# Layer 3 of a graph stack: another order for sums, W_h and W_out products, values and reciprocals within a period

## The chip, the cores and the metric

One core of a Trainium2 chip runs the whole program. The metric is the device time of one execution in microseconds, the median of several runs. Names in the profile: PE is the matmul engine, PEld its weight loader, DVE the vector engine, ACT the scalar engine, POOL the general one, SP the engine that here only issues DMAs. A "q" behind a name (SPq, ACTq) is the engine's instruction sequencer.

## The reference

Four graph layers follow each other on x (32 batches, 512 nodes, 64 features). Each takes h = relu(layernorm(x)) and adds its result to x. Only layer 3 is touched:

```python
def gat_layer(x, graph, W, b):
    h = x @ W
    s = jnp.einsum('bnd,bmd->bnm', h, h) * graph
    s = jnp.where(s == 0.0, NEG_INF, s)
    a = jax.nn.softmax(s, axis=2)
    return jnp.einsum('bnm,bmd->bnd', a, h) + b

heads = jax.vmap(lambda W, b: gat_layer(flow_x, graph, W, b))(Wh, bh)   # 8 heads, 64 -> 128
cat = jnp.moveaxis(heads, 0, 2).reshape(B, N, H * D)
x = jax.nn.leaky_relu(cat, negative_slope=0.01)
out = gat_layer(x, graph, W_out, b_out)                                 # 1024 -> 64
return jax.nn.leaky_relu(out, negative_slope=0.01)
```

## The kernel before

Layer 3 runs as a chain of 144 units. A `Heads` unit is two heads of one batch (32 batches x 4 = 128 units); an `Out` unit is the second attention of two batches (16 units). A unit handles k = 0, 1 (its two heads, or its two batches) side by side, in the two halves of the 128 rows or columns of PE. The 512 nodes are cut into C = 4 blocks of 128, so a unit has four score blocks, r = 0 to 3.

The steps of a unit, each a method of `Pair`, `Heads` or `Out`, on the engine named:

- `scores(r)` (PE): the 128 x 512 scores of block r, for both k. They go to a PSUM tile of the pool `ps_s`, which has two buffers (tag "s").
- `maxima(r)` (DVE, two instructions): adds the mask, takes the minimum of the negative along the row, writes the negated scores to `p_att`. After r = 3 the four blocks' maxima of both k stand in `top`.
- `spread_out` (DVE transpose, four SP DMAs to DRAM) and `spread_in` (one SP DMA of 512 KB): the maxima come back as a row on all partitions, `topb`.
- `shift(r)` (POOL): subtracts `topb`. The scores are symmetric, so a shift by the column's maximum serves.
- `exps(r)` (ACT): the exponential. For odd r it goes to PSUM, into one of the two buffers of `ps_s` (`e_ps`).
- `join(r)` for r = 1, 3 (DVE): p[r] = e_ps + p[r-1]. It frees the buffer in `ps_s`.
- `totals` (PE, then ACT): products with ones give the sums of each column, in a tile of the pool `ps_m` (two buffers, tag "m"); ACT copies them to `tot`. `totals_out`: two DMAs, one on SP and one on ACT, bring the two parts into `parts`, 128 partitions x 16.
- `values(j)` (PE): products of p[j] with the features, accumulated over j in `av`, the one buffer of `ps_v`. Since p[1] and p[3] are joined, even blocks use differences of features (`less_next`).
- `recips` (DVE): adds the two parts and takes the reciprocal; `recips_out` and `recips_in` (SP) send it through DRAM to all partitions, `recb`.
- `normalize` (DVE): o = av * recb. It frees `av`.
- A `Heads` unit goes on with `y_pe` (the two products with W_h, two tiles of `ps_m`), `y_act` (ACT: 0.01 y + 0.01 b_h) and `y_dve` (DVE: the maximum of that and y + b_h), which is `cat`. Two `Heads` units' `cat` feed `Out.product(h)` (PE): one head's share of the product with W_out, accumulated in `gT_ps` over the eight heads; `keep_product` (ACT) copies it out.
- An `Out` unit goes on with `y_act` (bias), `back` (PE: four transposes into a tile of `ps_m`; ACT: 0.01 y - 1), `back_dve` (DVE: the maximum), `back_pool` (POOL adds x) and `store` (SP).
- Preparations for later units: `features` (ACT, with one DVE reduction), `make_hx` (PE transposes in `ps_m`, ACT copy), `make_g` (PE: two products in `ps_m`, ACT copies), `make_v`, `make_gs`, `judge_product`.

The order is written by hand. The method `period(t)` (lines 711 to 769) lists what period t does for several units: `unit(k)` is the unit k places behind the one that now makes its scores. Under `manual_schedule` (line 1266) every engine, SP included, runs its instructions in the order in which this list issues them; the framework adds the waits and chooses which buffer of a pool a tile gets. An engine whose next instruction waits runs nothing behind it.

So in one period unit 0 makes score blocks 2 and 3 and their maxima, unit -1 its blocks 0 and 1, unit 1 its shifts, exponentials and joins, unit 2 its sums, values and reciprocals, unit 3 its normalisation, unit 4 the W_h product or the output. A product with W_out at period t takes the `cat` that unit 4 makes in the same period (first head of two), or the period before.

Of the kernel before, what the change touches and what calls it, by code (L numbers as in the profile page):

```python
# [8 lines left out]
F32 = mybir.dt.float32  # L9
# [5 lines left out]
P = 128  # L15
# [7 lines left out]
def fast_form(  # L23
# [25 lines left out]
    nc = tc.nc  # L49
    B, N, F = x.shape  # L50
    C = N // P
# [8 lines left out]
    tiny = ctx.enter_context(tc.tile_pool(name="tiny", bufs=4))  # L60
# [54 lines left out]
    for k in range(2):  # L115
        rows = slice(k * F, (k + 1) * F)
# [199 lines left out]
    class Pair:  # L316
# [112 lines left out]
        def totals(self):  # L429
            ps = ps_m.tile([P, N], F32, name="tot_ps", tag="m")  # L430
            for e in range(2):
                for k in range(2):
                    q = (2 * k + e) * 32
                    nc.tensor.matmul(  # L434
                        ps[q : q + 32, :], lhsT=ones, rhs=self.p[2 * e + 1][:, k],
                        start=True, stop=True,
                    )
            self.tot = wk.tile([P, N], F32, name="tot", bufs=1)
            nc.scalar.copy(self.tot, ps)  # L439

        def totals_out(self):

            self.parts = tiny.tile([P, 2, 8], F32, name="parts")
            rows = self.tot.rearrange("(k e r) n -> k e r n", k=2, e=2)
            for e, queue in enumerate((nc.sync, nc.scalar)):
                queue.dma_start(
                    self.parts[:, e], rows[:, e, 0].rearrange("k (g i) -> k g i", i=8)
                )

        def recips(self):  # L450
            self.rec = tiny.tile([P, 8], F32, name="rec_flow")
# [217 lines left out]
    def any_zero():  # L669

        def across(src, rows, name):
            ps = ps_m.tile([P, P], F32, name=name, tag="m")
            n = src.shape[0]
            nc.tensor.transpose(ps[:rows, :n], src, ident[:n, :n])
            return ps[:rows, :n]

        own = tiny.tile([P, 1], F32, name="own")
        nc.vector.tensor_reduce(own, least, AX.X, OP.min)
        two = tiny.tile([1, 2], F32, name="two")
        nc.vector.tensor_reduce(two[:, 0:1], across(own, 1, "own_ps"), AX.X, OP.min)  # L680
        best = tiny.tile([B // 2, 2], F32, name="best")
        nc.vector.tensor_reduce(
            best,
            across(least_out, B // 2, "out_ps").rearrange("b (k f) -> b k f", k=2),
            AX.X, OP.max,
        )
        worst = tiny.tile([B // 2, 1], F32, name="worst")
        nc.vector.tensor_reduce(worst, best, AX.X, OP.min)
        nc.vector.tensor_reduce(
            two[:, 1:2], across(worst, 1, "worst_ps"), AX.X, OP.min  # L690
        )
        flag = tiny.tile([1, 1], F32, name="flag")
        nc.vector.tensor_reduce(flag, two, AX.X, OP.min)
        nc.vector.scalar_tensor_tensor(
            again, flag, 0.0, unsound, op0=OP.is_equal, op1=OP.max
        )
# [6 lines left out]
    def planned(units, products):  # L703

        class Nothing:
            def __getattr__(self, name):
                return lambda *args: None

        nothing = Nothing()

        def period(t):
            def unit(lag):
                return units[t - lag] if 0 <= t - lag < len(units) else nothing

            now, ahead = unit(0), unit(-1)
            for r in range(2, C):
                now.scores(r)
            unit(3).recips_in()
            unit(4).y_pe()
            unit(1).shift(0)  # L720
            unit(1).exps(0)
            unit(4).y_act()
            u, h = products.get(t - 1, (None, 0))
            if u and h == H - 1:
                u.keep_product()
            unit(1).shift(2)
            unit(1).exps(2)
            for r in range(2, C):
                now.maxima(r)
            now.spread_out()  # L730
            now.spread_in()
            for r in range(2):
                ahead.scores(r)
            unit(4).y_dve()
            unit(3).normalize()
            for r in range(2):
                ahead.maxima(r)
            unit(4).back()
            unit(2).totals()
            unit(2).totals_out()  # L740
            unit(1).shift(1)
            unit(1).exps(1)
            u, h = products.get(t, (None, 0))
            if u:
                u.product(h)
            for j in range(C):
                unit(2).values(j)
            unit(1).join(1)
            unit(1).shift(3)
            unit(1).exps(3)  # L750
            unit(5).back_pool()
            unit(-2).make_gs()
            unit(2).recips()
            unit(2).recips_out()
            unit(5).store()
            unit(4).back_dve()
            unit(1).join(3)
            unit(-3).features(3)
            unit(-2).judge_product()
            unit(1).make_v()  # L760
            unit(-4).make_hx()
            unit(-2).make_g()
            for step in range(3):
                for lag, odd in ((step - 7, 0), (step - 11, 1)):
                    u = unit(lag)
                    if getattr(u, "i", None) == 0 and u.b % 2 == odd:
                        u.features(step)
            if t == len(units):
                any_zero()

        return period
# [1067 lines left out]
```

## Time and profile before

| what | us |
|---|---|
| median of 3 runs | 2101.37 |
| range of the 3 runs | 2099.18 to 2102.93 |
| profiled execution | 2099.58 |
| its span, first to last instruction | 2097.8 |
| first and last of the 144 transposes `top_t` | 460.7 and 2053.4 |

The clock granted to PE is 0.985 over the span. The durations of the steps, from the groups of the page and of the list by shape:

| line | step | engine | count | mean ns of one |
|---|---|---|---|---|
| L382 | maxima, one k | DVE | 1152 | 685 |
| L404 | shift | POOL | 576 | 2374 |
| L413 | exps to SBUF, to PSUM | ACT | 288, 288 | 1056, 1028 |
| L416 | join | DVE | 288 | 1203 |
| L439 | copy of the sums | ACT | 144 | 586 |
| L452, L455 | reciprocals | DVE | 144, 144 | 170, 203 |
| L472 | normalize | DVE | 144 | 683 |
| L563 | y_act of a `Heads` unit, one k | ACT | 256 | 680 |
| L571 | y_dve, one k | DVE | 256 | 737 |
| L652 | back_dve | DVE | 16 | 644 |

How to read it: a row of the timeline has the start, the time until the end of the last of the merged instructions, engine, line, operation, what it writes and reads, the count, and in brackets the idle time before with what ended it. Matmuls overlap, so their rate is read from distances of starts, not from their durations. An fp32 product shows as two matmul instructions, so the two products of a step (k = 0, 1) are "x4". DVE's instructions overlap a little too: I use the distances of starts in sums. A row of the windows has the stretch, its length, the busy time of PE, PEld, DVE, ACT and POOL with the instruction counts, PE's clock, the DMA share and GB/s. Bytes a packet and times of packets are from the trace's DMA records.

### The profile page before, as it was taken

The numbers are of one execution on the slowest core, as the hardware profiler recorded it, in microseconds if no ns is written. First come the engines' busy times: TensorE is split into PE (matmuls) and PEld (weight loads), VectorE is DVE, ScalarE is ACT, GpSimd is POOL, SyncE is SP. The second block draws the span as 40 slices with busy tenths as digits, with TensorE's granted clock in tenths as the row PEclk, the third lists the DMA queues.
The fourth block names the chain that finished last, engine by engine and source line by source line (L and its number), as shares of the span: only waits on it lengthen the run. The fifth ranks groups of instructions, "written<-read, shape, count | busy, mean of one in ns | idle before, by whom it ended". The sixth has DMA issues, their size and how long they took to land. (4 is left out here: it accounts for less than half of the span.)

```text
span 2097.8 us, 33009 instructions
## 1 busy us (share of the span) xinstructions
PE 2002.6 (95%) x11038; PEld 813.8 (39%) x11038; DVE 1786.2 (85%) x4257; ACT 1227.9 (59%) x1944; POOL 1432.7 (68%) x697
## 2 busy tenths in 40 slices
PE   7999999988999999999999999999999999999995
PEld 4667676652333333333333333333333333333321
DVE  6699997667998989898989898989888888988983
ACT  3444443335666666666666666666666666766553
POOL 3000000018898889888888988888888888888995
PEclk9999999989999999999999999999999999999998
DMA  5000000001222222222222222222222222222222
GB/s 139 1 1 2 1 2 1 1 22 57 77 75 69 78 77 73 78 76 82 68 78 77 72 77 77 77 71 74 68 77 73 77 67 73 77 71 74 77 68 78
DMA packets 135780, 129.35 MB, mean 62 GB/s; under 512 B 92792, under 2 KB 98080, under 8 KB 135472
## 3 DMA queue, kind: packets, MB, share of 16 engines
q1 hardware_dynamic: 116368, 126.35, 19.8%
q10 hardware_dynamic: 18720, 0.59, 0.5%
q8 instruction: 89, 1.46, 0.3%
q0 software_dynamic: 512, 0.20, 0.1%
q14 instruction: 91, 0.75, 0.1%
HBM read 119.48 MB, written 5.37 MB: 60 GB/s over the span
## 5 line engine op out<-in xcount | busy, mean ns | idle before, releaser
L404 POOL TENSOR_TENSOR p_att<-p_att,topb 128x1024 f32<-128x1024 f32 x576 | 1347.4, 2374 | 232.7 <-DMA topb<-top_row 130.6
L382 DVE CUSTOM_DVE_ANT_0 p_att<-s_ps,flow_neg 128x512 f32<-128x512 f32 x1152 | 727.8, 685 | 53.6 <-PE s_ps L370 51.9
L370 PE MATMUL s_ps<-hx,g 64*128 64x512 f32 x2048 | 545.3, 615 | 34.3 <-DVE p_att L416 24.6
L413 ACT ACTIVATE e_ps<-p_att 128x1024 f32<-128x1024 f32 x288 | 295.8, 1028 | 174.2 <-DVE top L382 107.8
L413 ACT ACTIVATE p_att<-p_att 128x1024 f32<-128x1024 f32 x288 | 304.2, 1056 | 149.6 <-POOL p_att L404 146.6
L416 DVE TENSOR_TENSOR p_att<-e_ps,p_att 128x1024 f32<-128x1024 f32 x288 | 346.5, 1203 | 24.7 <-ACT e_ps L413 24.4
L370 PEld LDWEIGHTS s_ps<-hx,g 64*128 64x128 f32 x2048 | 179.4, 186 | 343.1 <-DVE top L382 163.2
L422 PE MATMUL av<-p_att,hd 128*64 128x512 f32 x1024 | 264.3, 593 | 2.2 <-DVE o_att L472 2.0
L422 PE MATMUL av<-p_att,hn 128*64 128x512 f32 x1024 | 263.7, 592 | 0.0
L1053 POOL TENSOR_TENSOR x<-x,bias_b 128x512 f32<-128x512 f32 x16 | 20.3, 1271 | 280.0 <-DVE hn L826 280.0
L571 DVE SCALAR_TENSOR_TENSOR cat<-y_ps,bh,cat 128x512 f32<-128x512 f32 x256 | 178.1, 737 | 6.2 <-ACT cat L563 3.4
L563 ACT ACTIVATE cat<-y_ps,bh 128x512 f32<-128x512 f32 x256 | 161.7, 680 | 11.8 <-PE y_ps L553 8.7
L434 PE MATMUL tot_ps<-p_att,ones 128*32 128x512 f32 x1152 | 154.8, 610 | 1.6 <-DVE cat L571 0.5
L553 PE MATMUL y_ps<-o_att,wh_sb 64*128 64x512 f32 x512 | 143.2, 589 | 0.0
L598 PE MATMUL gT_ps<-cat,wo_sb 128*64 128x512 f32 x512 | 138.1, 618 | 0.0
L439 ACT COPY tot<-tot_ps 128x512 f32<-128x512 f32 x144 | 84.4, 586 | 85.0 <-PE tot_ps L434 83.6
L422 PEld LDWEIGHTS av<-p_att,hd 128*64 128x64 f32 x1024 | 73.2, 137 | 152.2 <-issue 141.2
L422 PEld LDWEIGHTS av<-p_att,hn 128*64 128x64 f32 x1024 | 74.8, 137 | 144.9 <-issue 144.9
L472 DVE TENSOR_TENSOR o_att<-av,recb 128x512 f32<-128x512 f32 x144 | 98.3, 683 | 34.9 <-DMA recb<-rec_row 34.6
L547 ACT COPY g<-g_ps 128x512 f32<-128x512 f32 x128 | 70.3, 588 | 95.3 <-PE g_ps L535 95.3
L977 PE MATMUL acc<-v,s 64*128 64x65 f32 x2048 | 124.1, 280 | 0.7 <-DVE s L963 0.4
L977 PEld LDWEIGHTS acc<-v,s 64*128 64x128 f32 x2048 | 121.2, 195 | 5.9 <-DVE o L993 1.2
(181 smaller groups left out, 2028.2 us busy)
## 6 DMA issues: line engine op xcount, KB each, us to landing
topb<-top_row SPq DMA_DIRECT2D x144, 512.0 KB
recb<-rec_row SPq DMA_DIRECT2D x288, 128.0 KB
top_row<-top_t SPq DMA_DIRECT2D x576, 1.0 KB
out_dram<-y SPq DMA_DIRECT2D x32, 128.0 KB
x<-in_x_dram SPq DMA_DIRECT2D x3, 1024.0 KB
parts<-tot ACTq DMA_DIRECT2D x144, 4.0 KB
parts<-tot SPq DMA_DIRECT2D x144, 4.0 KB
rec_row<-rec_flow SPq DMA_DIRECT2D x144, 4.0 KB
```

Of the source, the lines that this page charges most:

```text
L370: nc.tensor.matmul(ps[:, k], lhsT=g[halves(k), r * P : (r + 1) * P], rhs=x[halves(k), :], start=True, stop=True,)
L382: nc.vector.tensor_tensor_reduce(out=self.p[r][:, k], in0=ps[:, k], in1=flow_neg[:, r], scale=-1.0, scalar=BIG, op0=OP.add, op1=OP.min, ac ...
L404: nc.gpsimd.tensor_tensor(self.p[r], self.p[r], self.topb, OP.subtract)
L413: nc.scalar.activation(to, self.p[r], AF.Exp, scale=-1.0)
L416: nc.vector.tensor_tensor(self.p[r], self.joined, self.p[r - 1], OP.add)
L422: nc.tensor.matmul(self.av[halves(k), :], lhsT=self.v(k, j) if j % 2 else self.less_next(k, j), rhs=self.p[j][:, k], start=(j == 0), stop= ...
L434: nc.tensor.matmul(ps[q : q + 32, :], lhsT=ones, rhs=self.p[2 * e + 1][:, k], start=True, stop=True,)
L553: nc.tensor.matmul(ps, lhsT=wh_sb[halves(k), 2 * self.i + k, :], rhs=self.o[halves(k), :], start=True, stop=True,)
L563: nc.scalar.activation(self.cat[:, k], self.y[k], AF.Identity, bias=bh01[:, h : h + 1], scale=0.01)
L571: nc.vector.scalar_tensor_tensor(self.cat[:, k], self.y[k], bh[:, h : h + 1], self.cat[:, k], op0=OP.add, op1=OP.max,)
L598: nc.tensor.matmul(self.gps[halves(k), :], lhsT=wo_sb[:, h, :], rhs=Heads.cat.pop((self.b + k, h)), start=(h == 0), stop=(h == H - 1),)
L977: nc.tensor.matmul(self.acc[k][:, r], lhsT=self.s[b // 2][halves(k), b % 2, r * P : (r + 1) * P], rhs=self.v[halves(k), b], start=(b == 0) ...
```

## The change

Only order changes, and `totals_out` is cut in two: it issues one of its two DMAs, on the queue that it is given; `parts` is allocated in `totals`.

- `totals` of unit 2 goes from behind unit 4's `back` to a place behind exps(0): on PE between the unit's own score blocks and the blocks ahead, on ACT between exps(0) and exps(2). Its ACT DMA follows directly; its SP DMA goes between `spread_out` and `spread_in`.
- `y_pe` of unit 4 goes behind the blocks ahead; `y_act` behind exps(2).
- `y_dve` goes behind the maxima ahead, so normalize and these maxima come before it; `back_dve` directly follows.
- `values` goes in front of the product with W_out.
- `recips` and `recips_out` go in front of join(1).

```diff
             self.tot = wk.tile([P, N], F32, name="tot", bufs=1)
+            self.parts = tiny.tile([P, 2, 8], F32, name="parts")
             nc.scalar.copy(self.tot, ps)
 
-        def totals_out(self):
-
-            self.parts = tiny.tile([P, 2, 8], F32, name="parts")
+        def totals_out(self, e, queue):
+
             rows = self.tot.rearrange("(k e r) n -> k e r n", k=2, e=2)
-            for e, queue in enumerate((nc.sync, nc.scalar)):
-                queue.dma_start(
-                    self.parts[:, e], rows[:, e, 0].rearrange("k (g i) -> k g i", i=8)
-                )
+            queue.dma_start(
+                self.parts[:, e], rows[:, e, 0].rearrange("k (g i) -> k g i", i=8)
+            )
...
             unit(3).recips_in()
-            unit(4).y_pe()
             unit(1).shift(0)
             unit(1).exps(0)
-            unit(4).y_act()
+            unit(2).totals()
+            unit(2).totals_out(1, nc.scalar)
             u, h = products.get(t - 1, (None, 0))
...
             now.spread_out()
+            unit(2).totals_out(0, nc.sync)
             now.spread_in()
             for r in range(2):
                 ahead.scores(r)
-            unit(4).y_dve()
+            unit(4).y_pe()
+            unit(4).y_act()
             unit(3).normalize()
             for r in range(2):
                 ahead.maxima(r)
             unit(4).back()
-            unit(2).totals()
-            unit(2).totals_out()
+            unit(4).y_dve()
+            unit(4).back_dve()
             unit(1).shift(1)
             unit(1).exps(1)
+            for j in range(C):
+                unit(2).values(j)
             u, h = products.get(t, (None, 0))
             if u:
                 u.product(h)
-            for j in range(C):
-                unit(2).values(j)
+            unit(2).recips()
+            unit(2).recips_out()
             unit(1).join(1)
...
             unit(-2).make_gs()
-            unit(2).recips()
-            unit(2).recips_out()
             unit(5).store()
-            unit(4).back_dve()
             unit(1).join(3)
```

## The prediction

> **What bounds the kernel now.** The page's first table comes first, then the waits, then the period on each engine (timeline and windows).
>
> ```profile
> PE 2002.6 (95%) x11038; PEld 813.8 (39%) x11038; DVE 1786.2 (85%) x4257; ACT 1227.9 (59%) x1944; POOL 1432.7 (68%) x697
> ```
>
> The layer runs from about 460 us to the end in 144 periods, one a DVE transpose `top_t`; the mean distance of two is 11.14 us. A period is a unit's four score blocks, so I work per period. The list of waits (total us, times, longest):
>
> ```profile
> POOL p_att L404 <- DMA topb<-top_row: 130.6, 88, 3.4
> PEld tot_ps L434 <- DVE cat L571: 100.7, 128, 1.1
> DVE rec_flow L452 <- DMA parts<-tot: 77.1, 118, 2.4
> DVE o_att L472 <- DMA recb<-rec_row: 34.6, 34, 4.9
> PEld s_ps L370 <- DVE p_att L416: 126.3, 156, 10.2
> ```
>
> The change aims at lines 2 to 4. The busy time by window, for four whole periods (columns: length, then PE, PEld, DVE, ACT, POOL):
>
> ```profile
> 1213.85:1224.70 10.85, 10.81 (x53) 3.57 (x52) 10.04 (x25) 6.39 (x9) 9.15 (x5) 1.00 0.23 75
> 1258.03:1268.51 10.48, 9.88 (x44) 2.71 (x44) 9.73 (x25) 7.13 (x12) 9.30 (x6) 1.00 0.23 79
> 1268.51:1281.14 12.63, 11.90 (x52) 4.03 (x52) 9.12 (x24) 8.30 (x16) 11.49 (x6) 1.00 0.23 72
> ```
>
> PE and DVE are both nearly full, POOL not far behind. So the large wait of 100.7 us needs a look at what PE did meanwhile. The timeline of PE:
>
> ```profile
> 1211.82 1.02 PE L553 MATMUL y_ps<-o_att,wh_sb 64*128 64x512 f32 x4
> 1212.74 2.26 PE L370 MATMUL s_ps<-gs 64*128 64x512 f32 x8
> 1214.93 1.07 PE L434 MATMUL tot_ps<-p_att,ones 128*32 128x512 f32 x8
> 1215.93 1.08 PE L598 MATMUL gT_ps<-cat,wo_sb 128*64 128x512 f32 x4
> 1216.84 1.03 PE L422 MATMUL av<-p_att,hd 128*64 128x512 f32 x4
> 1219.41 1.03 PE L422 MATMUL av<-p_att,hn 128*64 128x512 f32 x4
> 1220.37 0.66 PE L298 MATMUL hx_ps<-ident,hs 128*128 128x128 f32 x4
> 1220.95 1.99 PE L370 MATMUL s_ps<-gs 64*128 64x512 f32 x8
> ```
>
> Products of one shape follow at 0.86 us a pair (1216.84 to 1219.41 is three). Around `tot_ps` PE loses only 0.1 us a period: the 100.7 us are the weight loader's, hidden by the matmul before. What is open on PE are the steps between shapes and the score blocks' waits. The page's worst place is the period with `back` (an output unit at lag 4) and `g`:
>
> ```profile
> 1274.75 1.12 PE L535 MATMUL g_ps<-hx,m 64*128 64x512 f32 x2
> 1276.55 0.69 PE L535 MATMUL g_ps<-hx,m 64*128 64x512 f32 x1 [0.68 <-ACT g L547]
> 1276.56 0.69 PE L370 MATMUL s_ps<-hx,g 64*128 64x512 f32 x1
> ```
>
> The second `g_ps` waits for the copy of the first: the two share one of `ps_m`'s two buffers, the other being held by `back_ps` until `back_dve`, late on DVE. 1.80 us instead of 0.96.
>
> **The Trainium skill.** *TensorEngine Tiling (Array Packing)*, Key Properties: changing the tiling mode drains TensorE. The trace agrees: 64*128 to 128*32 to 128*64 costs 0.05 to 0.14 us a step (1.00 and 0.91 in place of 0.86), 128*64 to the next shape 0.10 (0.96). *DMA: Bandwidth & Descriptors*, Queues, rings and completion order: descriptors of one queue are consumed in ring order. Here too: SP's `parts`, issued at 1216.87 behind `topb` (1216.43), has its packets at 1219.37 to 1219.82, when `topb`'s (from 1217.40) end at 1219.85. *Perfetto Trace Analysis*, Optimization Strategy: a gap that repeats on the full engine can mean that there isn't PSUM for the next tile; the second `g_ps` is such a gap.
>
> **Part by part: DVE.** Starts in the period from 1200.24: maxima, 2.57 later the transpose, 0.35 later the `cat` pair (1.46), normalize (0.61), the maxima ahead (2.46), join(1) (1.23), 0.38 idle for `parts`, the reciprocals (0.32), join(3) (1.09), `least_out` (0.59). Nothing is added or removed; only the idle time goes. In the new order: normalize at 2.92, maxima ahead 3.53, `cat` 5.99, reciprocals 7.45, join(1) 7.77, join(3) 9.00, end 10.09. This holds if each operand is there:
> - `parts` at 7.45. Both queues' issues come far earlier: ACT's about 2.6 to 3.1, SP's between the four `top_row` issues (end 4.1) and `topb` (about 5.1). SP idles there for the landing (131.5 us over the layer, some 0.9 a period), and the issue takes 0.57, so `topb` isn't delayed; the 128 packets of 32 B take 9 ns each, ahead of `topb`. Landing at about 6.1, spare 1.3. The cost if that cover goes: at most 0.57 on `topb`.
> - `recb` at 2.92 of the next period, 1.46 earlier than now. From reciprocal to landing the trace has 4.6 to 4.9 (1209.69 to 1214.5; 1220.64 to 1225.2). Landed at 12.4 to 12.7, wanted at 13.0 in the shortest period: spare 0.3. Late by x costs x, as the maxima ahead queue behind normalize.
> - the biases of `cat` (ACT) at 5.99: y_pe ends at about 4.5, two ACTIVATEs of 0.68 end at 5.95. Just in time. ACT's own queue: sum copy (0.59) and DMA issue (0.51) now lie between exps(0) and exps(2), where ACT waited for POOL; exps(1) ends at 7.0, join(1) wants it at 7.77.
> - exps(3): POOL's round is topb to shift 0 (transpose 1213.85 to 1220.36: 6.5), four shifts 9.4, exp 1.1, join 1.1, maxima 2.6: 20.7 for two periods. No pair of periods gets below that, 10.35 each.
>
> **PE.** From the first of a period's own scores (1209.99) to the second block ahead (1213.87) is 3.88 now, set by DVE's maxima. New: two blocks 0.96 + 0.86, sums 1.00, a step back to 64*128 that is new (0.1, plus 0.1 within the first block, as after any step to that shape: 0.20), first block ahead 0.86: 3.88. The added step fills what was slack. From there to the next scores: now 7.08; new 0.96 + W_h 0.86 + step 0.14 + values 3.43 + W_out 0.86 + step 0.10 + `hx` 0.58 = 6.93, since W_h to values is one step where sums and W_out needed two. Gain 0.15. The W_out product needs `cat`'s first half: done at 6.7, wanted at 8.1. The sums' buffer is free by then (the `g` copies end 1.3 after the first score block starts (1199.17, 1200.44), the sums come 1.8 after it).
>
> **Waits that are new, and who queues behind them.** The sums on PE wait for join(3); behind them stand the blocks ahead. But the unit's own second block, just before, waits for the same join (it frees that block's buffer), so this costs nothing. ACT's sum copy waits for PE's sums (done at about 2.0), and exps(2) stands behind it: its shift ends at about 3.0, the copy and the issue at 3.1. SP's `parts` waits for that copy (2.6) at 4.1, with `topb` behind it and POOL behind that; it would decide only if exps(0) came 1.5 later than now. The reciprocals on DVE wait for `parts` with join(1) behind them, and behind that the next period's first block: here lies what an error of the landing would cost, one for one beyond 1.3. The W_out product waits for `cat` at the end of PE's period, with 1.4 to spare. `back_dve` (0.64) goes where `cat` stands in other periods (1.46), so it isn't late for anything; `keep_product` moves with the product and has half a period more. In the last periods, after the final transpose (2053.4), the chain runs through shifts, exps, join, sums, `parts`, `recb`, `back` and the store, one unit alone; the order of others doesn't touch it, so its 44 us stay.
>
> **The sum**, by what PE does in a period (counts and means from the transposes):
> - 31 with `hx` or `gV`, 10.98 now: PE 0.15 (DVE needs 10.1 + 0.6): 4.7.
> - 46 with `g`, 11.19: PE-bound, 0.10: 4.6.
> - 41 with neither, 10.58: the wait for `parts` (0.66) goes, but PE's 10.1 and POOL's round are right behind: 0.20: 8.2.
> - 8 with `back` and `g`, 12.81: the second `g` (0.84), the `recb` wait (1.16 in the one from 1258) and a join behind ACT's sum copy (0.59). Their sum is 2.6, overlapping in part; the PE sum of such a period is 10.1. I take 1.7: 13.6. Bounds: 0.8 and 2.4.
> - 6 with `hx` and `g`, 12.6: 0.15; 12 at the ends: 0.2: together 3.3.
>
> 34.4 us. The profiled execution took 2099.6 (span 2097.8, 1.8 around it), so 2065 in its terms. It lies 1.8 under the median shown (2101.4): 2067.
>
> **Rivals.**
> - *Half the gain* (2080 to 2097): `recb` comes after its new due time, since its rec_row write now queues beside `topb`'s packets, or ACT is late with the biases. At 0.2 a period over 130 periods 26 us are lost: 2093. For: spare of 0.3 and none. Against: in the longer periods 0.9.
> - *Slower: the two `g` share a buffer everywhere.* `y_ps` now stays in `ps_m` until 7.45 of a period, where it was freed at 4.4; PE wants `g` at about 9. If the plan that deals out the two buffers believes `cat` later than that, each of the 60 periods with `g` gets the 0.84 that 8 have now: 52 x 0.84 = 44 more, and the 8 keep theirs (7): 2118. It turns slower than before once some 40 of them do. Against: spare 1.5 us by the trace.
> - *The change does nothing*: the new PE step is on the path and eats the rest. 0.2 x 140 = 28 against 34: 2095. For: PE is full; against: the maxima's slack.
>
> **How the numbers follow.** The forecast (2046 to 2080) 0.54; half the gain or nothing 0.24, of which 0.05 lies within 0.2%; slower 0.22, half of it beyond 2110. Within 0.2% (4.2 us) isn't told from no change. Range 2046 to 2110: low end from the upper bounds (O periods 2.4, plain periods 0.4: 14 more, and some), high end to half of the slower case. Faster 0.73, same 0.05, slower 0.22.
>
> **What would show it.** `rec_flow <- parts` near nothing; `g_ps <- ACT g` gone; the 12.6 us periods near 11; `tot_ps` followed by scores with a step of 0.2; `recb` waits not above 35 us. Wrong, if `o_att <- recb` or `g_ps <- ACT g` grow, or `topb` waits do.

## The result, and the profile after

| | before | after |
|---|---|---|
| median of 4 runs, us | 2102.15 | 2070.86 |
| range, us | 2099.18 to 2103.18 | 2070.20 to 2072.65 |
| profiled execution, us | 2099.58 | 2070.20 |
| its span, us | 2097.8 | 2068.4 |
| first, last transpose `top_t`, us | 460.7, 2053.4 | 459.8, 2022.2 |

The ratio is 0.9855, with an interval of 0.9838 to 0.9872: 31 us less, where 34 were forecast (2067). The clock granted to PE is 0.985 in both profiles. Busy time first, from the page's first table of the changed kernel:

```profile
PE 1982.9 (96%) x11038; PEld 808.1 (39%) x11038; DVE 1774.3 (86%) x4257; ACT 1220.4 (59%) x1944; POOL 1432.8 (69%) x697
```

The instruction counts are the same, yet PE's busy time fell by 19.7 us, more than its idle time (9.7): with the same products, a busy PE is no measure of its work. DVE's busy time fell by 11.9 and its idle time by 17.5. From the list of waits of the changed kernel (total us, times, longest):

```profile
POOL p_att L404 <- DMA topb<-top_row: 136.7, 93, 3.8
PEld back_ps L643 <- ACT o_att L638: 42.1, 15, 4.4
PE back_ps L643 <- ACT o_att L638: 30.0, 15, 3.8
DVE o_att L471 <- DMA recb<-rec_row: 23.1, 32, 5.6
DVE y L651 <- ACT y L648: 19.9, 14, 3.6
```

Three things stand there. The wait of the sums for `cat` (100.7) and of the second `g` for the copy of the first (12.0 on the loader, 5.4 on PE) have no line any more, and `rec_flow <- parts` went from 77.1 to 1.2. `topb` and `recb` are where they were, or lower (130.6 and 34.6 before). And one wait grew that the forecast hadn't: `back_ps <- ACT o_att`, on PE itself 7.9 us in 3 times before and 30.0 in 15 times now, with `y <- ACT y` behind it (1.5 before, 19.9 now). Two more waits of DVE grew: that of its joins for the exponentials, from 24.4 to 54.1 us, most of it before join(3), and that of its maxima for the scores, from 51.9 to 73.0.

The plain period (neither `hx`, `gV`, `g` nor `back`) now looks like this on PE, with one row of DVE; the windows ahead of it give the busy time of this period and of one with `back` and `g` (columns: length, then PE, PEld, DVE, ACT, POOL, clock, DMA share, GB/s):

```profile
1266.62:1276.75 10.13, 10.13 (x50) 3.19 (x48) 9.57 (x24) 6.61 (x12) 9.38 (x6) 1.00 0.38 107
1059.07:1071.33 12.26, 10.17 (x52) 3.40 (x48) 9.21 (x23) 8.60 (x16) 11.47 (x6) 1.00 0.22 66
```

```profile
1265.79 1.99 PE L370 MATMUL s_ps<-hx,g 64*128 64x512 f32 x8
1267.61 1.02 PE L552 MATMUL y_ps<-o_att,wh_sb 64*128 64x512 f32 x4
1268.56 1.08 PE L422 MATMUL av<-p_att,hd 128*64 128x512 f32 x4
...
1272.05 1.03 PE L597 MATMUL gT_ps<-cat,wo_sb 128*64 128x512 f32 x4
1273.01 1.99 PE L370 MATMUL s_ps<-hx,g 64*128 64x512 f32 x8
...
1274.18 0.69 DVE L382 CUSTOM_DVE_ANT_0 p_att<-s_ps,flow_neg 128x512 f32<-128x512 f32 x1 [0.49 <-PE s_ps L370]
...
1274.92 1.07 PE L434 MATMUL tot_ps<-p_att,ones 128*32 128x512 f32 x8
1275.92 1.99 PE L370 MATMUL s_ps<-hx,g 64*128 64x512 f32 x8
```

PE is busy for all 10.13 us of the plain period: no row of it carries a bracket with a wait, while DVE waits 0.49 us for the scores. The sums run between the own blocks and the blocks ahead, W_h directly behind these, the values next, W_out last. In the other window PE is busy for only 10.17 of 12.26 us.

Sorted by what PE does, the distances of the transposes give the account of the gain:

| period | count | mean before | mean after | gained, us | forecast, us |
|---|---|---|---|---|---|
| with `hx` or `gV` | 31 | 10.98 | 10.83 | 4.8 | 4.7 |
| with `g` | 46 | 11.19 | 11.08 | 5.1 | 4.6 |
| with neither | 41 | 10.58 | 10.38 | 8.0 | 8.2 |
| with `back` and `g` | 8 | 12.81 | 11.95 | 6.8 | 13.6 |
| `hx` and `g`; the ends | 6; 11 | 12.60; 11.45 | 12.43; 11.03 | 1.0; 4.6 | 3.3 for both |
| behind the last transpose | | 44.4 | 46.2 | -1.8 | 0 |

(The forecast counts 12 periods at the ends; 144 transposes leave 143 distances, and so 11.) With 0.9 from an earlier first transpose the gains make 29.4, the difference of the two spans. One row is off by half of its forecast: the period with `back` and `g`.

The means hide a spread. Of the 41 periods with neither, 27 gain 0.28 to 0.80 us (the median goes from 10.49 to 10.13), but five lose 0.5 to 1.15. The trace's DMA records show what stands ahead of these five. Two queues of the page (packets, MB, share of the DMA engines) bear the name "instruction" and carry none of the transfers named so far:

```profile
q8 instruction: 88, 1.44, 0.3%
q14 instruction: 90, 0.74, 0.1%
```

Of 132 periods, 41 have a packet of these queues between 1.0 and 3.0 us after the transpose, among the packets of `top_row`. SP issues `topb` 2.8 us after the transpose in the median; the 14 periods where it comes latest (3.3 to 4.7) are all among the 41, and without such a packet the latest is 3.2. Each of the five losers stands right behind one of the 14: POOL's shifts begin late there (8.62 us after the transpose in the worst, 6.63 in the median), and the next period's join waits for their exponentials. That these packets are the cause is read from the coincidence; no experiment moved them.

### The profile page after: what moved, and what is told of

Same layout as the page of the kernel before. It is cut to its first block, busy times and chain, and to the rows that moved or that the text cites. A ratio compares the mean times of both kernels' runs of the same rounds, so it can differ in the third digit from the quotient of the medians.

```text
span 2068.4 us, 32906 instructions
## 1 busy us (share of the span) xinstructions
PE 1982.9 (96%) x11038; PEld 808.1 (39%) x11038; DVE 1774.3 (86%) x4257; ACT 1220.4 (59%) x1944; POOL 1432.8 (69%) x697
## 5 line engine op out<-in xcount | busy, mean ns | idle before, releaser
L404 POOL TENSOR_TENSOR p_att<-p_att,topb 128x1024 f32<-128x1024 f32 x576 | 1347.8, 2375 | 202.1 <-DMA topb<-top_row 136.7
L370 PE MATMUL s_ps<-hx,g 64*128 64x512 f32 x2048 | 518.1, 615 | 21.8 <-DVE p_att L416 19.4
L416 DVE TENSOR_TENSOR p_att<-e_ps,p_att 128x1024 f32<-128x1024 f32 x288 | 342.4, 1200 | 55.4 <-ACT e_ps L413 54.1
L370 PEld LDWEIGHTS s_ps<-hx,g 64*128 64x128 f32 x2048 | 174.9, 186 | 336.7 <-DVE top L382 170.5
L422 PE MATMUL av<-p_att,hd 128*64 128x512 f32 x1024 | 270.5, 607 | 0.4 <-DVE o_att L471 0.4
L552 PE MATMUL y_ps<-o_att,wh_sb 64*128 64x512 f32 x512 | 133.0, 590 | 0.0
L597 PE MATMUL gT_ps<-cat,wo_sb 128*64 128x512 f32 x512 | 131.6, 592 | 0.0
L422 PEld LDWEIGHTS av<-p_att,hd 128*64 128x64 f32 x1024 | 62.3, 136 | 166.6 <-issue 130.1
L884 PE MATMUL nt_ps<-adj_t,hn 128*128 128x512 f32 x256 | 117.0, 600 | 0.8 <-DVE hn L848 0.8
L471 DVE TENSOR_TENSOR o_att<-av,recb 128x512 f32<-128x512 f32 x144 | 95.4, 663 | 23.8 <-DMA recb<-rec_row 23.1
```

Of the source, the lines that this page charges most:

```text
L370: nc.tensor.matmul(ps[:, k], lhsT=g[halves(k), r * P : (r + 1) * P], rhs=x[halves(k), :], start=True, stop=True,)
L404: nc.gpsimd.tensor_tensor(self.p[r], self.p[r], self.topb, OP.subtract)
L416: nc.vector.tensor_tensor(self.p[r], self.joined, self.p[r - 1], OP.add)
L422: nc.tensor.matmul(self.av[halves(k), :], lhsT=self.v(k, j) if j % 2 else self.less_next(k, j), rhs=self.p[j][:, k], start=(j == 0), stop= ...
L552: nc.tensor.matmul(ps, lhsT=wh_sb[halves(k), 2 * self.i + k, :], rhs=self.o[halves(k), :], start=True, stop=True,)
L597: nc.tensor.matmul(self.gps[halves(k), :], lhsT=wo_sb[:, h, :], rhs=Heads.cat.pop((self.b + k, h)), start=(h == 0), stop=(h == H - 1),)
```

## The experiments

### Where the time of the `back` periods goes

The timeline of one such period of the changed kernel, cut to what concerns `back`:

```profile
1058.52 1.06 ACT L413 ACTIVATE p_att<-p_att 128x1024 f32<-128x1024 f32 x1 [2.20 <-POOL p_att L404]
...
1060.83 1.06 ACT L413 ACTIVATE p_att<-p_att 128x1024 f32<-128x1024 f32 x1 [0.79 <-POOL p_att L404]
...
1061.80 0.71 ACT L638 ACTIVATE o_att<-o_att,b_out 128x512 f32<-128x512 f32 x1
...
1062.56 0.66 PE L643 MATMUL back_ps<-ident,o_att 128*128 128x128 f32 x4 [2.09 <-ACT o_att L638]
...
1066.73 1.13 PE L534 MATMUL g_ps<-hx,m 64*128 64x512 f32 x4
```

`back` transposes what ACT's bias (L638, the `y_act` of an `Out` unit) leaves in `o_att`. The change moved `y_act` behind exps(2). That step of ACT waits for POOL's second shift, until 1060.83, so the bias starts at 1061.80 and PE stands for 2.09 us with the values queued behind `back`. The operand of the bias had been there since the period before; only its place in ACT's order holds it. The two `g` products now run as one row (x4), without the 0.68 us between them that before has.

**The bias early** (e1): the `Out` unit's bias becomes a method of its own, called before exps(0), where ACT waits for POOL anyway. The `Heads` units keep their place.

```diff
+        def bias(self):
+            pass
...
-        def y_act(self):
+        def bias(self):
             nc.scalar.activation(self.o, self.o, AF.Identity, bias=b_out2, scale=1.0)
...
             unit(3).recips_in()
+            unit(4).bias()
             unit(1).shift(0)
             unit(1).exps(0)
```

> The changed kernel, but an output unit's bias (ACT, `y_act` of `Out`) stands in front of exps(0) instead of behind exps(2). Theory A (in the 16 periods with `back`, PE's transposes stand behind the blocks ahead and wait for this bias, which waits behind exps(2) for POOL's second shift): `back_ps <- ACT o_att` falls from 72 us of PE and weight-loader waits to under 15, the periods with `back` and `g` from 12.0 to about 10.8, time 2071 - 8 x 1.2 - about 6 in the last periods = 2055 (2048 to 2062). Rival B (those periods are set by POOL's round of shifts anyway): the wait goes, the period stays above 11.5, time 2066 to 2071.

Measured in 5 runs: 2061.27 (2060.16 to 2066.76), ratio 0.9812 (0.9798 to 0.9825). The intervals of this and of the changed kernel don't touch, so it is the fastest version of the study. Its waits, and the same two steps in its timeline:

```profile
PEld back_ps L646 <- ACT o_att L641: 6.6, 2, 5.4
PE back_ps L646 <- ACT o_att L641: 5.4, 2, 5.2
```

```profile
1051.83 0.70 ACT L641 ACTIVATE o_att<-o_att,b_out 128x512 f32<-128x512 f32 x1
...
1056.09 0.66 PE L646 MATMUL back_ps<-ident,o_att 128*128 128x128 f32 x4
```

The bias is done 3.6 us before `back`, which has no wait. The eight periods with `back` and `g` went from 11.95 to 10.65 on average, and the end behind the last transpose from 46.2 to 41.4, so the same wait had lengthened it too. Over all, the periods with `back` gave 10.0 and the end 4.8; the other periods lost 4.9 and the first transpose came 1.6 later: 8.4 us by the spans. Of the 4.9 lost, 4.6 lie in three periods right behind a shortened one: 10.13 to 12.06, 10.50 to 12.44, 10.13 to 10.86. Ahead of the first two stands the late `topb` described above: it is issued 4.75 and 4.40 us after the transpose, a 16 KB packet of q8 having ended at 3.3 and 3.0, where the last packets of `top_row` end too. The forecast's floor of 20.7 us for two periods on POOL does not explain them; two pairs of e1 lie below it (20.53 and 20.59). A holds; B's range begins above every run but the slowest.

**`back_dve` at its old place** (e2), the rest as changed:

```diff
             unit(4).y_dve()
-            unit(4).back_dve()
...
             unit(5).store()
+            unit(4).back_dve()
```

> The changed kernel with `back_dve` back in its old place, behind the reciprocals and the store, in front of join(3). Theory A (its early place is what gives the second `g_ps` a buffer of its own): the wait `g_ps <- ACT g` returns with the second `g` some 0.8 us late in the 8 periods with `back` and `g`, time 2071 + 3 to 7. Rival B (the early sums alone changed which buffer is dealt out): no such wait, 2071 or a little less, since DVE no longer waits for ACT's part of `back` (19.9 us in all).

Measured: 2073.41 (2066.09 to 2075.28), ratio 0.9868 (0.9853 to 0.9883), an interval that overlaps that of the changed kernel, so time does not tell them apart. The waits do (the profile is of the fastest of the four runs): `g_ps <- ACT g` has no line here either (B), `rec_flow <- parts` rose from 1.2 to 14.1, and `y <- ACT y` fell from 19.9 to 2.1. In the changed order the second `g` doesn't need `back_dve` early: in the period looked at, even the late one (1062.58) ends 0.1 before PE comes to `g` (1063.36), where before it started 0.36 behind the first `g` (1275.11 against 1274.75).

**`back_dve` early, alone** (e9): the kernel before, with this one line moved.

```diff
             unit(4).back()
+            unit(4).back_dve()
...
             unit(5).store()
-            unit(4).back_dve()
```

> The kernel before with `back_dve` alone moved directly behind the maxima ahead. Theory A (its late place holds `back_ps`'s buffer and makes the second `g_ps` wait in the 8 periods with `back` and `g`): that wait goes, 8 x 0.8 = 6 us less than before, 2095 to 2097. Rival B (the plan deals out the buffer by something else): `g_ps <- ACT g` stays at 12 us, time as before, 2100 to 2103.

Measured in 5 runs: 2084.81 (2081.91 to 2086.26), ratio 0.9921 (0.9907 to 0.9934). These are the lines that the kernel before has for it:

```profile
PEld g_ps L535 <- ACT g L547: 12.0, 8, 1.5
PE g_ps L535 <- ACT g L547: 5.4, 8, 0.7
```

Neither is in e9, and the eight periods went from 12.81 to 10.94: mechanism A. But its size is 16 us and not 6. A stall listed with 5.4 us on PE was worth 1.87 us in each of eight periods, 15 us. The starts of the single matmuls show why. The two products of a step (k = 0, 1) lie in the two halves of PE's rows and run side by side: in e9 both `g` start at 1264.76. In the kernel before, the first `g` runs alone (1274.75); when the second starts at 1276.55, the first score product runs beside it (1276.56), and the second score product only starts one step later, at 1277.51. DVE's maxima wait for both. Their row before, then in e9:

```profile
1278.57 0.69 DVE L382 CUSTOM_DVE_ANT_0 p_att<-s_ps,flow_neg 128x512 f32<-128x512 f32 x1 [1.69 <-PE s_ps L370]
```

```profile
1266.80 0.69 DVE L382 CUSTOM_DVE_ANT_0 p_att<-s_ps,flow_neg 128x512 f32<-128x512 f32 x1 [0.18 <-PE s_ps L370]
```

From the first `g` to this row it is 3.82 us before and 2.04 in e9, and the same within 0.02 in each of the eight periods: 0.84 is the late start of the scores, 0.94 the halves being out of step, 1.78 together. Half of the whole change's gain is to be had with one line.

### What the order of the rest is worth

**The SP part of the sums behind `topb`** (e3):

```diff
             now.spread_out()
-            unit(2).totals_out(0, nc.sync)
             now.spread_in()
+            unit(2).totals_out(0, nc.sync)
```

> The changed kernel with SP's `parts` issue behind that of `topb` again; the sums stay early. Theory A (it is the place on SP's queue ahead of the 512 KB, not the early sums, that brings the parts in time): the part lands with `topb`, 8.6 to 8.9 us after a period's first maxima, the reciprocals wait for it 1.2 to 1.5 us a period (`rec_flow <- parts` 150 us or more), join(1) and the next scores queue behind: 0.6 to 1.3 us a period, 2160 to 2260. Rival B (the sums' early time is enough): within 10 us of 2071.

Measured: 2185.92 (2181.45 to 2188.70), ratio 1.0405 (1.0389 to 1.0420). Its waits:

```profile
DVE rec_flow L451 <- DMA parts<-tot: 204.9, 131, 3.6
```

A in time and mechanism. One DMA issue past another turns a gain of 31 us into a loss of 84: 1.56 us on average in 131 periods at the reciprocals, with POOL's shifts then waiting for DVE (`p_att <- rec_flow`, 112.4 and 38.5). In three periods looked at, the packets of the 4 KB end 5.5 to 5.8 us after the transpose and those of `topb`'s 512 KB at 6.0 to 6.1; in the changed kernel the 4 KB end at 3.2 to 3.5, before `topb` starts. That fits the Trainium skill, *DMA: Bandwidth & Descriptors*, Queues, rings and completion order: each DMA engine consumes the descriptors of a queue in ring order. In front of `topb` the part costs nothing to be seen: SP's own list of waits of the changed kernel has

```profile
SPq L398 <- DMA top_row<-top_t: 40.3, 116, 2.2
```

where before it had 131.5. SP fills with the issue a time in which it had to wait for `top_row` to land.

**The reciprocals behind join(1)** (e4):

```diff
-            unit(2).recips()
-            unit(2).recips_out()
             unit(1).join(1)
...
             unit(5).store()
+            unit(2).recips()
+            unit(2).recips_out()
```

> The changed kernel with the reciprocals and their row behind join(1) again. Theory A (the place ahead of the join pays for `recb`, which normalize now wants 1.46 earlier): `recb` comes 1.2 later, `o_att <- recb` grows from 23 us to 50 to 90, in the short periods above all, time 2080 to 2100. Rival B (DVE has enough slack, the place doesn't matter): 2071 within 4, waits as they are.

Measured: 2094.34 (2091.76 to 2094.82), ratio 0.9961 (0.9946 to 0.9976). Two of its waits:

```profile
DVE o_att L471 <- DMA recb<-rec_row: 124.4, 125, 5.5
PEld av L422 <- DVE o_att L471: 85.8, 99, 2.2
```

A right in time and mechanism; the wait, expected at 50 to 90, is 124.4. Normalize moved to the front of the maxima ahead only pays because the reciprocals moved as well: some 22 us (0.9961 less 0.9855, times 2102) hang on 1.2 us of DVE's order.

**W_h and W_out moved, the sums not** (e5): on the kernel before, `y_pe`, `y_act`, `y_dve`, `back_dve` and `values` go to their new places; sums, their DMAs and the reciprocals stay.

```diff
-            unit(4).y_pe()
...
-            unit(4).y_act()
...
             for r in range(2):
                 ahead.scores(r)
-            unit(4).y_dve()
+            unit(4).y_pe()
+            unit(4).y_act()
...
             unit(4).back()
+            unit(4).y_dve()
+            unit(4).back_dve()
             unit(2).totals()
             unit(2).totals_out()
...
```

> The kernel before with the W_h and W_out steps moved alone: `y_pe` and `y_act` behind the blocks ahead, `y_dve` and `back_dve` behind the maxima ahead, the W_out product behind the values; sums and reciprocals stay where they were. Theory A (the parts of the change need each other: the early sums take PE's place between own blocks and blocks ahead, and leave the two `ps_m` buffers to `y_ps`): PE idles before the blocks ahead, and the sums wait for a buffer until `cat` is done, 6.7 us after the first maxima where PE wants them at 4.5; over 2 us a period, 2300 to 2450. Rival B (each part brings its share): 2080 to 2095.

Measured: 2523.00 (2520.59 to 2526.75), ratio 1.2014 (1.1995 to 1.2033), worse than either theory's range; the mechanism is A's. One wait of its list, and the place in its timeline:

```profile
PE tot_ps L434 <- DVE cat L571: 282.5, 128, 3.9
```

```profile
1212.80 1.02 PE L553 MATMUL y_ps<-o_att,wh_sb 64*128 64x512 f32 x4
1213.86 1.26 ACT L563 ACTIVATE cat<-y_ps,bh 128x512 f32<-128x512 f32 x2 [1.56 <-PE y_ps L553]
1214.95 1.41 DVE L571 SCALAR_TENSOR_TENSOR cat<-y_ps,bh,cat 128x512 f32<-128x512 f32 x2
1215.76 0.16 PEld L434 LDWEIGHTS tot_ps<-p_att,ones 128*32 128x32 f32 x8 [2.76 <-DVE cat L571]
1215.76 0.64 PE L434 MATMUL tot_ps<-p_att,ones 128*32 128x512 f32 x4 [1.93 <-DVE cat L571]
```

The W_h product fills both tiles of `ps_m`; the sums behind it need one, and it is free only when ACT and DVE have made the first `cat`. In the kernel before the same wait stood in the list with 100.7 us, but under PEld, and under PE with

```profile
PE tot_ps L434 <- DVE cat L571: 0.5, 2, 0.3
```

Here it is 282.5 under PE. It is not the whole loss: the granted clock is 0.965 in this kernel (0.985 to 0.987 for the kernel before, measured beside it), because it fell to half for 3.4 us in 35 places before the last transpose. That is 60 us at most, an estimate from 35 x 3.41 x 0.5.

**Sums and reciprocals moved, W_h not** (e6): on the kernel before, sums, both DMAs and the reciprocals go to their new places; `y_pe` stays ahead of the blocks ahead, directly behind the sums.

```diff
+            unit(2).totals()
+            unit(2).totals_out(1, nc.scalar)
+            unit(4).y_pe()
...
             now.spread_out()
+            unit(2).totals_out(0, nc.sync)
             now.spread_in()
...
             for j in range(C):
                 unit(2).values(j)
+            unit(2).recips()
+            unit(2).recips_out()
```

> The kernel before with sums, their DMAs and the reciprocals moved alone; the W_h product follows directly behind the sums on PE, still ahead of the blocks ahead, the W_out product stays ahead of the values. Theory A (the W_h product has to move for the buffers: its second half wants the buffer of the sums, which ACT frees behind exps(0) only): `y_ps` waits for ACT's copy some 0.7 us a period, and the blocks ahead come 1.5 later than now: 2120 to 2190. Rival B (the early sums are the whole gain): 2065 to 2080.

Measured: 2158.37 (2156.68 to 2159.50), ratio 1.0272 (1.0257 to 1.0288). Two of its waits:

```profile
DVE cat L570 <- ACT cat L562: 146.4, 128, 1.9
PEld y_ps L552 <- ACT tot L440: 74.1, 128, 1.4
```

A in time, and W_h behind the sums needs the tile that ACT's sum copy frees, in all 128 periods. But the wait that A names is the loader's; on PE itself 1.5 us of it are left. What costs is likely that ACT copies the sums before it comes to the biases, and that DVE, which here has `cat` in front of normalize and the maxima ahead, waits 1.14 us for it in each of 128 periods. The eight periods with `back` and `g` are 10.52 here, the shortest of all versions.

**W_out in front of the values** (e8), on the changed kernel:

```diff
-            for j in range(C):
-                unit(2).values(j)
             u, h = products.get(t, (None, 0))
             if u:
                 u.product(h)
+            for j in range(C):
+                unit(2).values(j)
```

> The changed kernel with the W_out product ahead of the values again. Theory A (it has to follow the values because `cat` now comes behind the maxima ahead): in every second period the product waits for the `cat` of the same period, 2.1 us later than PE gets there, 64 x 2.1 = 134: 2150 to 2230. Rival B (the place of the product does not matter): within 10 of 2071.

Measured: 2189.67 (2181.31 to 2193.15), ratio 1.0409 (1.0384 to 1.0434). Two of its waits:

```profile
PEld gT_ps L597 <- DVE cat L570: 121.3, 64, 3.1
PE gT_ps L597 <- DVE cat L570: 65.0, 64, 2.3
```

A in time. The 64 products that take the `cat` of their own period wait for it, 1.0 us on PE where A had 2.1; the other 64 don't. In the changed kernel the values stand between and no such wait is listed.

Put together: the W_h part alone costs 422 us, the sums alone 57, the change with W_out at its old place 89 against the kernel before, the reciprocals late 22 of the gain. All of them together give 31 us. Of the parts tried, only `back_dve` gains by itself.

## Why the prediction was right, and where it was not

Right, by its own steps:

- *DVE's idle time for `parts` goes*: 77.1 to 1.2, and e3 shows that it is the place ahead of `topb` that does it. The new order of DVE was worked out as 10.09 us and the plain period took 10.13, but that agreement is luck: less its wait for scores, DVE takes 9.64 of them, and PE fills the 10.13.
- *`topb` isn't delayed, SP idles there*: nearly so. SP's wait for `top_row` went from 131.5 to 40.3 and POOL's for `topb` from 130.6 to 136.7; the issue comes 2.9 us after the transpose on average, 2.7 before.
- *`recb` has 0.3 us to spare*: the wait fell from 34.6 to 23.1. e4, which puts the reciprocals 1.2 us later, takes the spare away and shows the predicted cost.
- *The biases of `cat` come just in time*: no wait of `cat` for ACT is listed (3.4 before); in e6, where ACT gets W_h at another moment, it is 146.4.
- *PE*: the sums followed by scores at a distance of 1.00 us, where 0.86 is the pace of one shape, cost nothing to be seen since the maxima's slack was there; 0.15, 0.10 and 0.20 a period gave 4.8, 5.1 and 8.0 us where 4.7, 4.6 and 8.2 had been worked out. The plain periods stop where PE is full. Their 0.20 is right as a mean only: the median gains 0.36, and five long periods take the rest back.
- *The 100.7 us of the sums' wait are the loader's*: its end didn't bring 100 us.
- *W_out has 1.4 us to spare behind the values*: no wait for `cat`, and e8 shows what it is without them.

The rivals fell: `recb` and ACT's `cat` are on time (half the gain), the two `g` share no buffer (slower), and the new step of PE was covered (nothing).

**What failed** is the term of the sum for the eight periods with `back` and `g`, "I take 1.7: 13.6", which measured 0.85 and 6.8, and with it "so its 44 us stay" for the end, which became 46.2. Two errors of opposite sign are in it, and from the transposes and starts they add up to the measured 0.85:

- The second `g`'s stall was priced by the distance that it opens on PE, 0.84. It costs 1.78, since the scores behind it run out of step (e9); from the first `g` to the maxima the changed kernel has the same 2.04 as e9.
- A wait was missed that comes with the change. The step "ACT's own queue" was worked out for the biases of `cat` alone. An `Out` unit's bias moves with the same call, from behind exps(0) to behind exps(2), and PE's `back` needs it right behind the blocks ahead: 30.0 us on PE in 15 places. The first `g` comes 7.35 us after the transpose on average, 6.42 before, a loss of 0.93, although normalize's wait for `recb` in these periods went from 1.51 to 0.22 as forecast. e1 shows it: with the bias in front of exps(0) these periods take 10.65, and the gain there is 17 us (12.81 less 10.65, by 8), more than the 13.6 forecast.

So the total came out near by luck: the 6.8 lost here were partly made up at the ends (1.0 and 4.6 for 3.3) and by the earlier first transpose (0.9). POOL's floor of 20.7 us for two periods was no floor either: it takes 6.5 from the transpose to the first shift, which runs from 6.0 to 8.1 in the kernel before. The attribution of the `g` gain to `back_dve` holds for the kernel before (e9), but not for the changed one: there e2 puts it back and no `g` waits.

Left open: whether moving the packets of the "instruction" queues, which stand ahead of the long periods, would win their time back.

## What to carry to other kernels

When a call in a hand-written order is moved, list what it stands for in each kind of unit: here one `y_act` was two steps, the frequent one had its place chosen, the rare one lost 2 us each time because its operand had long been ready and its queue was not. Orders that share a two-buffer pool have to be moved as a whole; single parts of a good change may each be worse than the start, so test a part by taking it out of the whole as well as by doing it alone. And a wait in the weight loader's row says little about PE: 100.7 us there stood beside 0.5 us on PE. A stall on PE can cost more than the list has for it: 5.4 us were worth 15, because two products that should run side by side were parted.

## What the runs showed that was not expected

A stop of PE can lower its clock, and the length of the stop alone does not decide it. In the period from 958 us of the changed kernel `back` waited 2.37 us for the bias; then the clock fell. The windows of it:

```profile
950.00:961.90 11.90, 9.60 (x46) 2.77 (x44) 11.00 (x29) 7.60 (x12) 9.91 (x6) 1.00 0.23 69
961.97:964.00 2.03, 2.03 (x8) 0.85 (x10) 0.92 (x4) 1.34 (x2) 2.03 (x2) 0.70 0.73 256
964.00:966.00 2.00, 2.00 (x8) 0.64 (x6) 1.45 (x4) 1.20 (x2) 2.00 (x2) 0.50 0.04 4
966.00:968.00 2.00, 2.00 (x12) 0.53 (x10) 1.17 (x1) 0.00 (x0) 2.00 (x2) 0.95 0.31 77
```

The third column from the right is the granted clock: 1.00, then 0.70 and 0.50 as means of two windows, and back to 0.95. The trace's clock records have it at half for 3.41 us. The pairs of values ran 1.6 to 1.7 us apart in place of 0.86, and the period took 13.99 us; the other seven of its kind, which waited there for 1.04 to 2.09 us and kept a clock of 1.00, took 11.66 on average. Not all of these 2.33 us are the clock's: in e1, where `back` does not wait and the clock stays up, the same period is also longer than its seven likes, 11.66 to 10.51, behind a late `topb`.

The Trainium skill has the fall to half in *TensorE: Matmul & The Clock Gate*, Part 1, but after an idle window of some 3.4 us; here an idle time of 2.37 us was enough, and the measurement decides. The other traces say more. In e3 a wait of 1.93 us (593.4) was followed by a fall, in e5 one of 2.77 (1155.6) was not. In every trace the changes of the clock lie on one grid of 3.41 us, to within 2 ns. So I took PE's busy share in each step of that grid, in all ten traces, from 500 us to the last transpose. Of 22 steps with a share below 0.42 at full clock, all 22 were followed by half a clock for the next step; of 49 between 0.42 and 0.48, 27; of 4563 above, none. The step ahead of the fall shown has 0.31; the 2.77 us in e5 lay across two steps. What counts, then, is how much of one step PE stands still; for a wait of some 2 us that depends on where in the grid it falls.
